# Scores of graph edges: one-hot products for all slots instead of gathers for 54 of them, with GpSimd taking every second group

## The chip, the cores and the metric

The kernel runs on one core of a Trainium2 chip. Its time is the device time of one execution in microseconds (us); smaller is better. The engines are TensorE (PE; its weight loads are shown as PEld), VectorE (DVE), ScalarE (ACT), GpSimd (POOL) and SyncE (SP, which here only issues DMAs). All of them run beside each other and wait for each other by semaphores; each works through its own queue in order. PE writes to PSUM banks, which DVE and ACT can read.

## The reference

Four layers are applied to 1250 nodes with 768 features, each as `x = x + layer(layernorm(x))`: a graph attention with 12 heads, a mixture of 8 experts, a graph attention with 3 relations (two convolutions, of 4 heads and of 1), and an attention block with routing. There are 20,000 edges, sorted by destination. What matters here is the score of an edge, which each of the three graph convolutions needs before its softmax:

```
e = leaky_relu(a1[src] + a2[dst])            # layer 0, 12 heads
qi = xr[etype, dst] @ q;  kj = xr[etype, src] @ k
alpha = leaky_relu(qi + kj)                  # layer 1, 4 heads and 1 head
```

Then come a maximum over each destination's edges, the exponential, the sum over each destination, and the sum of the weighted source rows.

## The kernel before, in words

**Tiles and slots.** Nodes lie in 10 tiles of 128. Edges are packed by destination tile into `NS` = 172 slots of 128 edges. A slot belongs to one destination tile; its sources are anywhere. For each slot there are two rows in DRAM, `lo_rows` (source modulo 128) and `dl_rows` (destination within its tile), and on the chip `hi_f` (source tile) or `key_f` (source tile and relation).

**`edge_weights` (L418 to L617)** computes the scores. It is called three times: g0 for layer 0 (L774), g1 and g2 for the two convolutions of layer 1 (L1211, L1255). It works in blocks of `step` slots, 18 in g0 and g1, 32 in g2. In a block:

- SP loads `row_lo` and `row_dl`, each spread over 128 partitions (L494), and DVE compares them with the partition's number (L495): one-hot matrices in bf16.
- *Source scores, one-hot.* PE multiplies a slot's one-hot matrix with the scores of all source tiles, split into three bf16 parts (L507, `p_al`), so that every edge gets the scores of its source for all 10 tiles (times 3 relations). A group of `ag` = 4 slots (16 in g2) fills a PSUM bank, two groups a pair of banks. DVE multiplies the group with the one-hot choice of the tile, `sel_k` (L473), into `c_al` (L514) and sums over the tiles (L516, `s_a`). A block of 18 slots has five groups: four of 480 columns and one of 240.
- *Source scores, gathered.* Where `al_d` is given (g0 and g1), this is left out for the first `GATHERED` = 54 slots. Their scores are fetched by 54 indirect DMAs of GpSimd (L468, `gal`) from a table in DRAM, which SP writes tile by tile (L718 `al_d`, L1202 `al1_d`). The 118 other slots are done first, the 54 in the last three blocks.
- *Destination scores.* PE multiplies `row_dl` with the scores of the slot's own tile (L523, `p_ar`); ACT and DVE add the three parts into `d_e` (L529 to L531).
- The two are added (L550 for gathered slots, L558 or L560 for the others) and go through the leaky relu into `e` (L566).
- At the third block the penalties that end a segment are made (L403 to L414) and loaded (L539 to L545).
- `fill(beside)` (L567): in g1 and g2 each block also issues products of layer 1's values, `xr` (L1141), one node tile and relation at a time, 24 matmuls each, followed by ACT's copy to `v_r` (L1153) and SP's write to the table (L1154). 20 of them are left for g1 and the stretch behind it.

Behind the blocks come the two scans for the segment maximum and the exponential (L568 to L616), then `aggregate` (L619), whose gathers read the tables.

**Between the experts and g1 (L1192 to L1202)** `combine` gathers each node tile's two expert outputs `y` by GpSimd (L1084) and DVE adds them to `xs` (L1087); the tile is normed, turned by PE and multiplied with the first relation's weights (`xr`, L1141). At the fifth tile (`t == 4`) the weights `wr` of the two other relations are loaded by SP, four DMAs of 1152 KB (L1121), inside `issue_after(added.ins)` (L1197), which orders only instructions of the same engine as `added`, DVE, behind it.

The order of instructions on an engine is set at build time by a scheduler that goes by program order and its own estimates; a queue then runs in that order whatever happens. PSUM has three pairs of banks for `p_al`, `xr` and others, and two single banks for `p_ar`.

Of the kernel before, what the change touches and what calls it, by code (L numbers as in the profile page):

```python
# [8 lines left out]
F32 = mybir.dt.float32  # L9
# [6 lines left out]
N = 1250  # L16
# [3 lines left out]
NREL = 3  # L20
# [23 lines left out]
RUNS = {H0: 18, H1: 6, 1: 2}  # L44
GATHERED = 54
ES = (2 * N + NEXP * 127) // 128
# [24 lines left out]
class Fast:  # L71
# [345 lines left out]

    def edge_weights(self, name, nrel, heads, al, ar, s, al_d=None, bufs=(2, 2),  # L418
                     fill=lambda n: None, beside=0):


# [4 lines left out]
        nk = NT * nrel  # L426
        ng = GATHERED if al_d is not None else 0
        per = RUNS[heads]
        rows = NSP // per
        hr = rows * heads  # L430
        with tc.tile_pool(name=name + "_m", bufs=1) as rp:
# [8 lines left out]
            with tc.tile_pool(name=name + "_w", bufs=1) as wp:  # L440
# [22 lines left out]
                parts(ar, "arp", arp, lambda o, q: o[:, :, q])  # L463
                gal = None
                if ng:
                    gal = wp.tile([128, ng, g], F32, name="gal")
                    for j in range(ng):
                        nc.gpsimd.indirect_dma_start(  # L468
                            out=gal[:, j, :], out_offset=None, in_=al_d,
                            in_offset=bass.IndirectOffsetOnAxis(ap=self.src_i[:, j:j + 1], axis=0))  # L470
                sel = wp.tile([128, NS - ng, nk], BF16, name="sel_k")
                key = (self.hi_f if nrel == 1 else self.key_f)[:, ng:]
                nc.vector.tensor_tensor(sel, self.iota[:, None, :nk].to_broadcast([128, NS - ng, nk]),  # L473
                                        key[:, :, None].to_broadcast([128, NS - ng, nk]), op=ALU.is_equal)
                if nrel > 1:
# [9 lines left out]
                step = 18 if g > 3 else 32  # L485
                for s0 in list(range(ng, NS, step)) + list(range(0, ng, step)):
                    n = min(step, NS - s0)
                    hot = {}
                    for nm, lists in (("lo", self.lo_rows), ("dl", self.dl_rows)):
                        if nm == "lo" and s0 < ng:  # L490
                            continue
                        w = wp.tile([128, step * 128], BF16, name="row_" + nm, bufs=bufs[nm == "dl"])
                        flat = lists[s0:s0 + n].rearrange("s e -> (s e)")
                        nc.sync.dma_start(w[:, :n * 128], flat[None, :].to_broadcast([128, n * 128]))  # L494
                        nc.vector.tensor_scalar(w[:, :n * 128], w[:, :n * 128], self.own, None,  # L495
                                                op0=ALU.is_equal)
                        hot[nm] = w
                    for i, j0 in enumerate(range(0, n if s0 >= ng else 0, ag)):
                        m = min(ag, n - j0)
                        if i % 2 == 0:  # L500
                            pair = self.ps2("p_al")
                        p = pair[:, i % 2]
                        for j in range(j0, j0 + m):
                            lhs = hot["lo"][:, j * 128:(j + 1) * 128]
                            o = p[:, (j - j0) * nk * heads:(j - j0 + 1) * nk * heads]
                            for q in range(3):
                                mark = nc.tensor.matmul(o, lhs, alp[q].rearrange("p h t r -> p (h t r)"),  # L507
                                                        start=q == 0, stop=q == 2)
                        marks.append(mark)
                        c = wp.tile([128, ag, heads, nk], F32, name="c_al", bufs=2)  # L510
                        v = p[:, :m * nk * heads].rearrange("p (s h k) -> p s h k", s=m, h=heads)
                        ss = slice(s0 + j0, s0 + j0 + m)
                        so = slice(s0 + j0 - ng, s0 + j0 + m - ng)
                        nc.vector.tensor_tensor(c[:, :m], v, sel[:, so, None, :].to_broadcast(  # L514
                            [128, m, heads, nk]), op=ALU.mult)
                        nc.vector.tensor_reduce(sa[:, ss], c[:, :m], AX.X, ALU.add)  # L516
                    for j0 in range(0, n, bg):
# [13 lines left out]
                        nc.vector.tensor_add(o, o, v[:, :, 2])  # L531
                    if s0 == ng + 2 * step:
                        with tc.issue_after(marks[-1].ins):
                            self.penalties(heads)
                        pen = self.pen[heads]
                        rows_in = (sep[:, :per * 128], self.sep_rows), (loss[0], pen[0]), (loss[1], pen[1])
                        for i, (dst, src) in enumerate(rows_in):
                            v = src.rearrange("(r b) e -> r (b e)", b=per)
                            nc.sync.dma_start(dst, v[None].to_broadcast([heads, rows, per * 128]))  # L539
                            if i:  # L540
                                c = per * 128 - 1 if i == 1 else 0
                                ends = rp.tile([1, rows], BF16, name=f"ends{i}")
                                nc.sync.dma_start(ends, v[:, c:c + 1].rearrange("r o -> o r"))
                                nc.vector.tensor_copy(edge[:, i - 1],
                                                      ends[:, None, :].to_broadcast([1, heads, rows]))  # L545

                    b = slice(s0, s0 + n)
                    o, db = sa[:, b], d[:, b]
                    if s0 < ng:
                        nc.vector.tensor_add(db if nrel > 1 else o, db, gal[:, b])  # L550
                    if nrel > 1:
                        dv = db.rearrange("p s (r h) -> p s r h", r=nrel)
                        nc.vector.tensor_tensor(dv, dv, rsel[:, b, :, None].to_broadcast(
                            [128, n, nrel, heads]), op=ALU.mult)
                        if s0 < ng:
                            nc.vector.tensor_add(o, dv[:, :, 0], dv[:, :, 1])
                        for r in range(2 if s0 < ng else 0, nrel):
                            nc.vector.tensor_add(o, o, dv[:, :, r])  # L558
                    elif s0 >= ng:
                        nc.vector.tensor_add(o, o, db)  # L560
# [121 lines left out]
    def layer0_values(self, pp):  # L682

        nc, const, wf = self.nc, self.main, self.wf
        self.tab0 = self.dram.tile([N, H0 * (F0 + 1)], F32, name="tab0")
        self.al_d = self.dram.tile([N, H0], F32, name="al_d")
        self.alr = const.tile([128, NT, 2, H0], F32, name="alr0")
# [20 lines left out]
    def node_values(self, v0, t):  # L708
# [6 lines left out]
        for i in range(2):  # L715
            nc.scalar.copy(self.alr[:r, t, i].rearrange("p (b k s) -> p b k s", b=2, k=3),
                           v[:, :, :, 128 + 2 * i:130 + 2 * i])
        nc.sync.dma_start(self.al_d[rows_of(t)], self.alr[:r, t, 0])  # L718
        for b in range(2):
# [41 lines left out]
    def layer0_graph(self):  # L761
        nc, tc = self.nc, self.tc
        hns, self.pen = {}, {}
        with tc.tile_pool(name="g0e", bufs=1) as ep, ExitStack() as path:
            e0 = self.slot_rows(ep, "e0", H0)
            with tc.tile_pool(name="g0p", bufs=1) as pp:
# [5 lines left out]
                for _ in tiles:  # L772
                    pass
                marks = self.edge_weights("g0", 1, H0, self.alr[:, :, 0], self.alr[:, :, 1], e0, self.al_d,  # L774
                                          (4, 6))
                self.layer0_residuals(pp, self.hT0, marks)
# [335 lines left out]

    def load_relations(self, pool, w, bufs, rels=range(NREL), ng=0):

        nc, a = self.nc, self.a
        ws = []
        for r in rels:
            for n, (o, wd) in enumerate(HALF):
                x = ng if r == 0 and n == 0 else 0
                t = pool.tile([128, KD, 384 + x], F32, name="wr0" if x else "wr", bufs=1 if x else bufs)  # L1120
                nc.sync.dma_start(t[:, :, :384], a[w][r].rearrange("(k p) f -> p k f", p=128)[:, :, o:o + wd])  # L1121
                ws.append(t)
# [44 lines left out]
    def layer1_graph(self):  # L1167
        nc, tc, a, xs, dram = self.nc, self.tc, self.a, self.xs, self.dram
        g1, g2 = NREL * H1, NREL
        with ExitStack() as path:  # L1170
# [9 lines left out]
            tab2 = dram.tile([NREL * N, D + 1], F32, name="tab2")  # L1180
            al1_d = dram.tile([N, NREL * H1], F32, name="al1_d")
            al1 = hp.tile([128, NT, g1], F32, name="al1")
# [6 lines left out]
            with tc.tile_pool(name="g1x", bufs=1) as xp:  # L1189
                vs = self.value_rows(xp, H1, F1)  # L1190
                with tc.tile_pool(name="moec", bufs=1) as cp:
                    for t in range(NT + 1):  # L1192
# [3 lines left out]
                        if t == 4:  # L1196
                            with tc.issue_after(added.ins):  # L1197
                                ws += self.load_relations(xp, "L1_gnn_W1", 4, (1, 2))
                        if t:
                            m = rows_of(t - 1)  # L1200
                            self.relation_values(vs, hT, ws, t - 1, 0, H1, F1, tab1, al1, ar1)
                            nc.sync.dma_start(al1_d[m], al1[:ROWS[t - 1], t - 1, :])  # L1202
                moe.close()
# [6 lines left out]
                fill = self.filler(vs, hT, ws, H1, F1, tab1, al1, ar1)  # L1210
                self.edge_weights("g1", NREL, H1, al1, ar1, e1, al1_d, fill=fill, beside=1)  # L1211
                for t in range(NT):
# [1314 lines left out]
```

## Time and profile before

| what | value |
|---|---|
| median of 7 runs | 2313.34 us (2305.57 to 2321.84) |
| the profiled execution's own time | 2315.46 us |
| its span | 2313.4 us |
| PE busy | 2081.5 us, 90% |
| DVE busy | 1253.7 us, 54% |
| POOL busy | 905.7 us, 39% |
| ACT busy | 302.0 us, 13% |
| g0: blocks of slots | 55 to 132 us of the span |
| `y` gathers to the first `xr` | 718 to 737.5 us |
| g1: blocks of slots | 825 to 942 us |
| rest of the fillers, to the next gather | 942 to 1029.8 us |
| g2: blocks of slots | 1381 to 1491 us |

Where the time goes is told by stage, since different engines set the pace in different stages. These are rows of the table by stretch: bounds in us from the span's start, length, then busy time and number of instructions of PE, PEld, DVE, ACT and POOL, the clock granted to PE (1.00 is full), the mean busy share of the 16 DMA engines and GB/s.

```profile
55.00:131.00 76.00, 49.68 (x642) 46.16 (x642) 60.12 (x153) 10.22 (x28) 54.58 (x54) 0.77 0.51 156
...
720.00:800.00 80.00, 65.31 (x224) 39.63 (x225) 42.42 (x92) 12.46 (x26) 28.92 (x37) 0.87 0.49 184
...
870.00:940.00 70.00, 66.71 (x445) 43.10 (x442) 38.32 (x106) 7.16 (x19) 28.75 (x32) 0.98 0.37 103
```

In g0 no engine is busy throughout, in g1 PE nearly is. Other views used further on are the timeline (start, duration, engine, line, operation, and in brackets the idle time of the engine before it with what ended it), the waits (who waited for whom: total, times, longest) and the chain of work that ended last.

### The profile page before, as it was taken

What the parts mean: (1) busy time and instruction counts of PE and PEld (TensorE: products, weight loads), DVE (VectorE), ACT (ScalarE), POOL (GpSimd) and SP (SyncE); (2) the same over time, 40 slices, a digit from 0 to 9 for tenths busy, and PEclk for the clock granted to TensorE, in tenths of its full rate; (3) what the DMA queues carried; (4) which work ended last, traced back from release to release, by engine and by line L of the source; (5) the groups of instructions that cost most, each with busy time, mean ns of one, the idle gap of its engine ahead of it and who ended that gap; (6) DMA issues with size and microseconds to landing.
All of it is one profiled execution on the core that took longest, in us unless ns stands there. A gap on an engine that the chain in (4) does not pass through costs nothing.

```text
span 2313.4 us, 25705 instructions
## 1 busy us (share of the span) xinstructions
PE 2081.5 (90%) x9261; PEld 1306.1 (56%) x9261; DVE 1253.7 (54%) x2548; ACT 302.0 (13%) x619; POOL 905.7 (39%) x930
## 2 busy tenths in 40 slices
PE   4659999779996999979999989989999999999868
PEld 4544445457774656545555546645555555656556
DVE  7877778889714376618667634112456601244371
ACT  3020000112221100100000010000001100122141
POOL 3748888422104154117777610017765000130040
PEclk9779999979997999989999999999999999999889
DMA  6558898589997164539876525339997010420141
GB/s 215 154 177 260 288 314 280 187 308 383 361 317 264 45 197 108 170 128 338 267 229 219 185 88 186 110 116 311 337 318 279 22 51 0 137 101 6 49 134 55
DMA packets 155930, 445.14 MB, mean 192 GB/s; under 512 B 38525, under 2 KB 75762, under 8 KB 154512
## 3 DMA queue, kind: packets, MB, share of 16 engines
q0 software_dynamic: 55200, 252.50, 33.0%
q1 hardware_dynamic: 95488, 178.02, 22.4%
q10 hardware_dynamic: 5104, 12.85, 1.5%
q8 instruction: 77, 1.26, 0.2%
q14 instruction: 61, 0.50, 0.1%
HBM read 381.43 MB, written 61.87 MB: 192 GB/s over the span
## 4 chain that ended last, share of the span: by engine, by line
PE 55%; DMA 5%; DVE 5%; issue 3%; ACT 1%; POOL 1%; SPq 0%; POOLq 0%; DVEq 0%; ACTq 0%
PE xr L1141 18%; PE acc L654 8%; PE acc L656 8%; PE mix L1395 4%; PE pv L1395 3%; PE pk L1558 3%; PE av L1599 2%; PE pl L1569 2%; PE pf L1684 2%; DMA x_mid<-xs 2%; DMA row<-tab,rel_i 1%; PE ph L1675 1%; PE p_al L507 1%; PE pT L1584 1%; PE mix L1508 1%
## 5 line engine op out<-in xcount | busy, mean ns | idle before, releaser
L633 POOL DMA_INDIRECT row<-tab,rel_i x344 | 387.6, 1127 | 351.2 <-DMA tab<-v_r 169.2
L1141 PE MATMUL xr<-wr,hT 128*128 128x384 f32 (+4 forms) x1440 | 488.1, 496 | 7.5 <-DVE c_al L514 3.9
L1141 PEld LDWEIGHTS xr<-wr,hT 128*128 128x128 f32 (+1 forms) x1440 | 268.9, 190 | 198.8 <-issue 42.4
L650 DVE TENSOR_TENSOR msg<-row,e 128x780 f32<-128x780 f32 (+1 forms) x344 | 328.0, 962 | 97.7 <-DMA row<-tab,src_i 48.8
L654 PE MATMUL acc<-msg,hots 128*128 128x390 f32 (+3 forms) x688 | 290.1, 503 | 35.4 <-DVE msg L650 21.3
L656 PE MATMUL acc<-msg,hots 128*128 128x390 f32 (+3 forms) x688 | 283.9, 493 | 0.0
L633 POOL DMA_INDIRECT row<-tab,src_i x172 | 219.6, 1277 | 78.0 <-DVE e L615 25.8
L654 PEld LDWEIGHTS acc<-msg,hots 128*128 128x128 f32 (+1 forms) x688 | 123.5, 189 | 145.6 <-DVE msg L650 51.2
L656 PEld LDWEIGHTS acc<-msg,hots 128*128 128x128 f32 (+1 forms) x688 | 130.8, 191 | 93.6 <-issue 7.8
L1109 DVE CUSTOM_DVE_ANT_0 wjunk<-wrow,qb 128x768 f32<-128x768 f32 x180 | 160.6, 947 | 12.7 <-DMA wrow<-in_L_gnn_W_dram 12.7
L654 PE MATMUL acc<-row,hot 128*128 128x384 f32 (+1 forms) x344 | 140.1, 489 | 8.8 <-DMA row<-tab,rel_i 8.8
L468 POOL DMA_INDIRECT gal<-al_d,src_i x108 | 112.5, 1042 | 79.0 <-issue 54.4
L656 PE MATMUL acc<-row,hot 128*128 128x385 f32 (+1 forms) x344 | 140.0, 489 | 0.0
L1040 PEld LDWEIGHTS ph<-xT,w 128*128 128x128 f32 x864 | 107.0, 196 | 30.0 <-ACT gT L1043 13.9
L638 DVE TENSOR_SCALAR hot<-iota,dloc,e 128x128 f32<-128x128 f32 x172 | 59.9, 354 | 112.1 <-PE acc L656 92.7
L1040 PE MATMUL ph<-xT,w 128*128 128x128 f32 x864 | 114.0, 283 | 5.6 <-DMA w<-in_L_ffn_w_dram 3.8
L1153 ACT COPY v_r<-xr 128x768 f32<-128x768 f32 (+1 forms) x60 | 47.9, 798 | 449.2 <-PE xr L1141 201.3
L1050 PE MATMUL mo<-w,gT 128*128 128x384 f32 x288 | 103.7, 488 | 0.0
L654 PEld LDWEIGHTS acc<-row,hot 128*128 128x128 f32 (+1 forms) x344 | 64.7, 191 | 53.5 <-issue 12.4
L507 PE MATMUL p_al<-alp,row_lo 128*128 128x120 bf16 (+1 forms) x1224 | 68.4, 214 | 29.2 <-DVE c_al L514 13.4
L656 PEld LDWEIGHTS acc<-row,hot 128*128 128x128 f32 (+1 forms) x344 | 65.4, 190 | 46.2 <-issue 2.8
L507 PEld LDWEIGHTS <-row_lo 128*128 128x128 bf16 x1224 | 63.5, 106 | 42.8 <-issue 25.7
(419 smaller groups left out, 2440.1 us busy)
## 6 DMA issues: line engine op xcount, KB each, us to landing
w<-in_L_ffn_w_dram SPq DMA_DIRECT2D x48, 1152.0 KB
wr<-in_L_gnn_W_dram SPq DMA_DIRECT2D x12, 1152.0 KB
wrow<-in_L_gnn_W_dram POOLq DMA_DIRECT2D x36, 384.0 KB, 6.3
tab<-v_r SPq DMA_DIRECT2D x27, 386.0 KB
tab<-v_r SPq DMA_DIRECT2D x27, 384.5 KB
row_dl<-dl_rows SPq DMA_DIRECT2D x18, 576.0 KB
y_d<-y ACTq DMA_DIRECT2D x24, 384.0 KB
row_lo<-lo_rows SPq DMA_DIRECT2D x12, 576.0 KB
```

The source lines that it names most:

```text
L468: nc.gpsimd.indirect_dma_start(out=gal[:, j, :], out_offset=None, in_=al_d, in_offset=bass.IndirectOffsetOnAxis(ap=self.src_i[:, j:j + 1], ...
L507: mark = nc.tensor.matmul(o, lhs, alp[q].rearrange("p h t r -> p (h t r)"), start=q == 0, stop=q == 2)
L633: nc.gpsimd.indirect_dma_start(out=row, out_offset=None, in_=table, in_offset=bass.IndirectOffsetOnAxis(ap=idx[:, s:s + 1], axis=0))
L650: nc.vector.tensor_tensor(msg.rearrange("p (h f) -> p h f", h=heads), row.rearrange("p (h f) -> p h f", h=heads), es[:, :, None].to_broadc ...
L654: nc.tensor.matmul(acc[:r, 0, :cut], hot[:, :r], msg[:, :cut], start=b == 0, stop=b == CAP[t] - 1)
L656: nc.tensor.matmul(acc[:r, 1, :w - cut], hot[:, :r], msg[:, cut:], start=b == 0, stop=b == CAP[t] - 1)
L1040: nc.tensor.matmul(p[:, o], w1[:, k, f * 128:(f + 1) * 128], xT[:, k // 3, (k % 3) * T:(k % 3 + 1) * T], start=k == 0, stop=k == KD - 1)
L1050: nc.tensor.matmul(p[:, n, :w], gT[:, f * T:(f + 1) * T], w2[:, f, o:o + w], start=f == 0, stop=f == 2)
L1109: nc.vector.tensor_tensor_reduce(out=junk, in0=wr, in1=qb[:, i, h, :], scale=1.0, scalar=0.0, op0=ALU.mult, op1=ALU.add, accum_out=out[:, ...
L1141: nc.tensor.matmul(p[:m, n, :w.shape[2]], hT[:, k, rows_of(t)], w[:, k, :], start=k == 0, stop=k == KD - 1)
L1395: self.nc.tensor.matmul(p[:m, n, :384], left(k), ws[n][:, k, :], start=start and k == 0, stop=k == ks - 1)
L1558: nc.tensor.matmul(p[:, :w], wk[o // 3][:, k, (o % 3) * 128:(o % 3 + 1) * 128], hT[:, k, c:c + w], start=k == 0, stop=k == KD - 1)
```

## The change

1. `GATHERED`, the tables `al_d` and `al1_d`, their writes and the gathers `gal` are gone. All 172 slots get their source scores by one-hot products, in their natural order; `sel_k` covers all slots.
2. Of the groups of a block, those with an odd number are copied from PSUM to `c_al` by ACT and multiplied there by GpSimd; the even ones stay with DVE. DVE sums all of them. `c_al` has three buffers instead of two. This holds in g0, g1 and g2.
3. In `load_relations` each weight tile is first written in one element by DVE, queued behind the fifth tile's sum, so that the load has to wait for that write.

```diff
-GATHERED = 54
...
-                for s0 in list(range(ng, NS, step)) + list(range(0, ng, step)):
+                for s0 in range(0, NS, step):
...
-                    for i, j0 in enumerate(range(0, n if s0 >= ng else 0, ag)):
+                    for i, j0 in enumerate(range(0, n, ag)):
...
-                        c = wp.tile([128, ag, heads, nk], F32, name="c_al", bufs=2)
+                        c = wp.tile([128, ag, heads, nk], F32, name="c_al", bufs=3)
...
-                        nc.vector.tensor_tensor(c[:, :m], v, sel[:, so, None, :].to_broadcast(
-                            [128, m, heads, nk]), op=ALU.mult)
+                        if i % 2:
+                            nc.scalar.copy(c[:, :m], v)
+                            v = c[:, :m]
+                        (nc.gpsimd if i % 2 else nc.vector).tensor_tensor(
+                            c[:, :m], v, sel[:, ss, None, :].to_broadcast([128, m, heads, nk]), op=ALU.mult)
                         nc.vector.tensor_reduce(sa[:, ss], c[:, :m], AX.X, ALU.add)
...
-    def load_relations(self, pool, w, bufs, rels=range(NREL), ng=0):
+    def load_relations(self, pool, w, bufs, rels=range(NREL), ng=0, behind=None):
...
+                if behind is not None:
+                    with self.tc.issue_after(behind.ins):
+                        nc.vector.memset(t[:1, 0, :1], 0.0)
                 nc.sync.dma_start(t[:, :, :384], a[w][r].rearrange("(k p) f -> p k f", p=128)[:, :, o:o + wd])
...
-                            with tc.issue_after(added.ins):
-                                ws += self.load_relations(xp, "L1_gnn_W1", 4, (1, 2))
+                                ws += self.load_relations(xp, "L1_gnn_W1", 4, (1, 2), behind=added)
```

## The prediction

> **What bounds** the kernel now: I began with the page (TensorE, "PE", is busy for 90% of the span), then read the chain that ended last, the timeline of the three stages that the change touches, the waits of PE, and the tables by stretch. "g0", "g1" and "g2" are the three calls of `edge_weights`.
>
> In g0 (55 to 132 us) no engine is full; the end is set by the 54 gathers of `gal`. These are lines of the timeline, columns start, duration, engine, line, operation, with the idle time before in brackets:
>
> ```profile
> 126.99 0.94 POOL L468 DMA_INDIRECT gal<-al_d,src_i  x1 [0.30 <-issue]
> 128.24 0.94 POOL L468 DMA_INDIRECT gal<-al_d,src_i  x1 [0.30 <-issue]
> ...
> 124.97 0.44 DVE L531 TENSOR_TENSOR d_e<-d_e,p_ar 128x168 f32<-128x168 f32 x2
> 130.75 0.38 DVE L550 TENSOR_TENSOR s_a<-d_e,gal 128x216 f32<-128x216 f32 x1 [5.33 <-DMA gal<-al_d,src_i]
> 131.17 0.54 DVE L566 SCALAR_TENSOR_TENSOR e<-s_a 128x216 f32<-128x216 f32 x1
> ```
>
> GpSimd (POOL) issues a gather each 1.25 us (0.94 + 0.30) from 58.45 on. VectorE (DVE) is through at 125.4 and waits 5.33 us for the last one. So at most 5.3 us are to be had before DVE itself is late.
>
> In g1 (825 to 942) PE is the bound. Each block of 18 slots ends with one `xr` product of the filler, and ScalarE's copy of it marks the blocks:
>
> ```profile
> 838.38 0.80 ACT L1153 COPY v_r<-xr 128x768 f32<-128x768 f32 x1 [8.75 <-issue]
> 853.76 0.80 ACT L1153 COPY v_r<-xr 128x768 f32<-128x768 f32 x1 [12.46 <-issue]
> 868.39 0.80 ACT L1153 COPY v_r<-xr 128x768 f32<-128x768 f32 x1 [11.61 <-issue]
> 880.01 0.80 ACT L1153 COPY v_r<-xr 128x768 f32<-128x768 f32 x1 [8.22 <-issue]
> 895.80 0.80 ACT L1153 COPY v_r<-xr 128x768 f32<-128x768 f32 x1 [8.81 <-issue]
> 907.42 0.80 ACT L1153 COPY v_r<-xr 128x768 f32<-128x768 f32 x1 [8.54 <-issue]
> 917.13 0.80 ACT L1153 COPY v_r<-xr 128x768 f32<-128x768 f32 x1 [8.31 <-PE p_ar L523]
> 925.41 0.80 ACT L1153 COPY v_r<-xr 128x768 f32<-128x768 f32 x1 [7.17 <-issue]
> 933.68 0.80 ACT L1153 COPY v_r<-xr 128x768 f32<-128x768 f32 x1 [7.17 <-issue]
> ```
>
> An undisturbed block with one-hot source scores takes 11.62 us (868.39 to 880.01, and 895.80 to 907.42), a gathered block 8.27 us. The other three took 15.38, 14.63 and 15.79. From 942 the fillers run on without a gap to 1025.9, and the next stage waits for the last table write. So a microsecond of PE in g1 is a microsecond of the span. In 824.7 to 1025.9 PE was busy 189.26 of 201.20 us: the 11.9 us idle is all that can hide anything.
>
> Between the experts and g1 (718 to 737) the chain of waits starts with a gather:
>
> ```profile
> 719.24 6.67 DMA y<-y_d,pos_i
> ...
> 737.75 9.57 PE xr L1141 x24
> ```
>
> **Part 1**, source scores of 54 more slots in g1: 54 slots of three products; by the blocks, 3 x (11.62 - 8.27) = +10.05 us of PE. What was removed there (54 gathers, 10 writes of `al1_d` of 0.32 us on SP's queue, three adds of 0.38 us on DVE) lay beside PE and gives nothing. `sel_k` for 172 instead of 118 slots costs DVE 5.53 - 3.85 = 1.7 us (g2 and g1 rows) at 808, beside 16 us of `xr`; if that cover went, it would be 1.7 us.
>
> **Part 2**, odd groups through ScalarE and GpSimd, in g1. The slow blocks' excess is 3.76 + 3.01 + 4.17 = 10.9 us, of which the penalties' products (861.9 to 864.2, 2.3 us) stay, so at most 8.7 us can go. PE's waits name the cause:
>
> ```profile
> PE xr L1141 <- DVE c_al L514: 3.9, 3, 2.5
> PE p_al L507 <- DVE c_al L514: 3.1, 1, 3.1
> ```
>
> That is 7.0 us in which PE waits for DVE to empty a bank of scores. At 841.4 DVE stood 1.82 us before a `row_lo` load with an odd group's product queued behind it; ScalarE (11 us busy of 117) would have emptied that bank in about 0.55 us (its 512-column copy of `p_run` takes 0.586). But the even groups of each bank pair stay on DVE. I take 4.0 of the 8.7. So g1 costs +10.05 - 4.0 = +6.0 us, with ends of +1.3 and +10.05.
>
> **Part 3**, g0: GpSimd's gathers go and DVE is what is late next. DVE is busy 60.8 of the 76.7 us between 55.0 and 131.7. Added: three `row_lo` comparisons, 3 x 0.80 = 2.4; reductions of 12 full and 3 half groups, 12 x 0.60 + 3 x 0.35 = 8.25 (back-to-back rows). Products on DVE fall from 26 full and 7 half to 19 and 10: 19 x 0.61 + 10 x 0.36 = 15.2 against 18.4, -3.2. The `gal` adds turn into `d_e` adds of the same 0.37. Net +7.4, busy 68.2. Idle was 15.9, less the gather wait 5.33 = 10.6. With those gaps kept g0 ends at 55.0 + 68.2 + 10.6 = 133.8: +2.1 us. PE's extra 54 x 3 products (12 in 0.71 us, 1.36 at half clock: 10 to 18 us) go into 27 us in which PE was idle here. `sel_k` (+0.6 us) lies before 55, where DVE waits 1.96 us for ScalarE's `alr`; `al_d` writes of 0.32 us leave SP's queue there, at most -0.5 us, taken as nothing.
>
> The gaps: about 4.5 us of the 10.6 belong to the penalties (80 to 85, and waits for their DMA), the other 6 to PE; I take half of those away with the freed banks, -3. Against that stands a new collision. GpSimd's product of 480 columns is not in the trace; its 768-column add takes 1.81 us, so 480/768 of it gives 1.13, I take 1.2. And while GpSimd computes, some DVE instructions stand still:
>
> ```profile
> 2224.87 1.80 POOL L1669 TENSOR_TENSOR xs<-xs,xb 128x768 f32<-128x768 f32 x1 [0.45 <-DVE ln_rs L117]
> 2225.23 1.86 DVE L118 TENSOR_SCALAR hn<-xs,ln_mv,ln_rs 128x768 f32<-128x768 f32 x1
> ...
> 2227.17 1.82 POOL L1669 TENSOR_TENSOR xs<-xs,xb 128x768 f32<-128x768 f32 x1 [0.50 <-DVE hn L118]
> 2227.48 2.33 DVE L1662 TENSOR_TENSOR xs<-xs,ya 128x768 f32<-128x768 f32 x1
> ```
>
> `hn` takes 0.67 us alone, the sum of two SBUF tensors 0.96; here both end only after GpSimd's add, +1.2 and +1.4. A reading of PSUM beside it (L1368, 0.40) was not stretched. So the exposed ones in a block are the two comparisons, the `s_a` add and L566: 2.5 us of some 8. Two products of 1.2 us cover 0.3 of a block; 4 instructions x 0.3 x half a product (0.6) = 0.7 us per block; by the order of the queue (product, reduction, then the exposed ones) I take half, 0.35 x 9.5 = +3.4. Ends: 0, and half a product for each of the 19, +11.4. So g0 costs 2.1 - 3 + 3.4 = +2.5 us, with ends of -3.9 and +13.5.
>
> The Trainium skill, "GPSIMD Engine Reference", section "Engine selection", speaks against this part: elementwise work belongs on VectorE, since GpSimd is about twice as slow with two inputs. The rows agree with the ratio (1.81 against 0.95 us). Followed, the rule would put 19 x 0.61 = 11.6 us back on DVE in g0 and leave out the +3.4: 8.2 us worse here, because GpSimd has nothing else to do in this stage once the gathers are gone.
>
> **Part 4**, the weights behind the fifth sum: in the old kernel the block had no effect: SP issued the four `wr` loads at 717.81, before the first sum at 724.54, and the 16 DMA engines were full (share 1.05, 416 GB/s at 722 to 724) while the first `y` gathers waited 6.67 us to land. Now a one-element DVE write after the fifth sum (741) holds the loads back. Four such writes cost 0.3 us on DVE, hidden by `xr`; behind the waiting loads on SP's queue stands the first `tab` write (749), which may slip some 2 us and has three buffers. First use of these weights is 829.6. With quiet engines a gather lands in 3.8 (`ya`, least) to 4.8 us (`row`, median); the DVE chain behind it moves as a whole. This gives 4.8 - 6.67 = -1.9 us, with ends of 0 and 3.8 - 6.67 = -2.9.
>
> g2 gets five odd groups and no more slots; PE runs `xr` there for 15 us at a stretch: 0.
>
> **Sum**: +6.0 + 2.5 - 1.9 = +6.6. On the profiled execution (span 2313.4, 2.06 around it, 2315.46) that is 2322; on the median of seven, 2313.34, it is 2320, and that is my number.
>
> **Rivals**:
> *The gaps close.* ScalarE frees the banks early, so g1's three slow blocks become normal (+1.3), g0 loses all 6 us of gaps and meets no collision (2.1 - 6 = -3.9), and the gather lands in 3.8 (-2.9): -5.5, 2308. For it: the 7.0 us of PE's waits on DVE. Against it: every bank pair keeps an even group on DVE, whose queue still waits for loads. It decides from the point where g1's excess over 11.62 us per block is under 2 us in all.
> *The shared access.* GpSimd's products stop DVE at L495, L566 and the adds for half a product each time in g0, +11.4, and DVE then empties banks no sooner in g1, so nothing is recovered: 10.05 + 13.5 - 1.9 = +21.7, 2335. For it: the two stretched rows. Against it: the products fall where DVE reduces. It decides once L495 in g0 has a mean over 1.1 us (now 0.80).
> *The held-back loads give nothing,* since the DVE chain of the first two tiles (726 to 736) is reordered or the loads now cross the later gathers: forecast + 1.9 = 2322.
>
> **Chances**: forecast 0.47, gaps close 0.25, shared access 0.20, loads give nothing 0.08. The forecast's own range is 2314 to 2326. A difference of 0.3% (6.9 us) is about what can be told from no change: under 2306.4 lies somewhat less than half of "gaps close" (0.11); over 2320.3 lie half of the forecast, all of "shared access", most of the last (0.48); between them 0.41. The range 2306 to 2332 leaves out about a tenth on each side.
>
> **Checks**: right are ten blocks of 11.6 us or more in g1, but for the short last one; the first gather after g1 6.6 us later than 1029.8; last L566 of g0 at 133 to 136; the first `y` landing in under 5.2 us. Wrong would be g1 blocks of 10 us, g0 ending before 129, or a stretched DVE op while GpSimd is idle.

## The result, and the profile after

The changed kernel takes 2324.86 us (median of 18 runs, 2317.49 to 2332.67) against 2313.28 us of the kernel before (46 runs beside them): ratio 1.0055, 95% interval 1.0042 to 1.0068, so +12.7 us (+9.7 to +15.7). The forecast was +6.6. The profiled execution took 2326.39 us, its span is 2324.7.

Line numbers after the change are lower by 9 to 16: `row_lo` is compared at L483, `p_al` is L495, ScalarE's copy L503, the product `c_al` L505, its sum L507, `p_ar` L514, `e` L553, the row gathers L620, `xr` L1129, `v_r` L1141.

**g0.** Rows of the table by stretch (columns as before: bounds, length, busy time and count of PE, PEld, DVE, ACT, POOL, clock, DMA share, GB/s), then waits of DVE in g0 (total, times, longest; the first two lines before, the other two after), then the timeline where the scores end and where the row gathers begin:

```profile
56.00:139.90 83.90, 54.35 (x753) 49.79 (x754) 67.72 (x168) 17.26 (x43) 20.81 (x19) 0.78 0.39 128
...
870.00:940.00 70.00, 69.70 (x589) 47.92 (x587) 46.44 (x117) 13.87 (x31) 12.70 (x12) 1.00 0.34 118
```

```profile
DVE c_al L514 <- PE p_al L507: 5.9, 9, 1.1
DVE s_a L550 <- DMA gal<-al_d,src_i: 5.3, 1, 5.3
...
DVE s_a L507 <- POOL c_al L505: 9.9, 13, 1.8
DVE c_al L505 <- PE p_al L495: 2.4, 3, 1.7
```

```profile
138.31 0.65 DVE L507 TENSOR_REDUCE s_a<-c_al 128x48 f32<-128x480 f32 x1 [0.95 <-POOL c_al L505]
139.00 0.28 DVE L547 TENSOR_TENSOR s_a<-s_a,d_e 128x120 f32<-128x120 f32 x1
139.32 0.37 DVE L553 SCALAR_TENSOR_TENSOR e<-s_a 128x120 f32<-128x120 f32 x1
```

```profile
168.57 1.78 POOL L1083 DMA_DIRECT2D qb<-in_L_gnn_q_dram  x3 [26.68 <-DVE e L602]
170.66 1.04 POOL L620 DMA_INDIRECT row<-tab,src_i  x1 [0.30 <-ACT e L603]
```

The last score is ready at 139.7 in place of 131.7 us. In place of one wait of 5.33 us for a gather, DVE now waits 13 times for a product of GpSimd, 9.9 us in all. The first row gather goes out 11.0 us later than before (170.66 against 159.64): 8.0 us of this lie ahead of the last score and 3.0 behind it, where among others three loads of `qb` now stand ahead of the gather.

**g1.** PE is busy for 69.70 of 70 us at the full clock (second row above). The fillers' copies, as in the prediction:

```profile
868.48 0.80 ACT L1141 COPY v_r<-xr 128x768 f32<-128x768 f32 x1 [8.85 <-PE xr L1129]
880.04 0.80 ACT L1141 COPY v_r<-xr 128x768 f32<-128x768 f32 x1 [6.59 <-PE xr L1129]
891.60 0.80 ACT L1141 COPY v_r<-xr 128x768 f32<-128x768 f32 x1 [6.59 <-PE xr L1129]
903.15 0.80 ACT L1141 COPY v_r<-xr 128x768 f32<-128x768 f32 x1 [6.59 <-PE xr L1129]
```

From 868 to 938 each block takes 11.56 us; there is no block of 8.3 any more, and only the first three are longer (13.58, 12.32, 15.07).

**The `y` gathers**, issue to landing; least, median and most were 6.0, 6.7 and 7.4 before:

```profile
DMA to landing us min/median/max: 3.7/4.7/8.9
```

### The profile page after: what moved, and what is told of

Read it like the earlier page. It is cut to its first block, busy times and chain, and to the rows that moved or that the text cites. A ratio compares the mean times of both kernels' runs of the same rounds, so it can differ in the third digit from the quotient of the medians.

```text
span 2324.7 us, 26287 instructions
## 1 busy us (share of the span) xinstructions
PE 2096.5 (90%) x9585; PEld 1324.2 (57%) x9585; DVE 1271.7 (55%) x2575; ACT 326.4 (14%) x662; POOL 835.0 (36%) x865
## 4 chain that ended last, share of the span: by engine, by line
PE 56%; DVE 5%; DMA 5%; issue 2%; ACT 1%; POOL 1%; SPq 0%; DVEq 0%; ACTq 0%; POOLq 0%
PE xr L1129 19%; PE acc L643 7%; PE acc L641 7%; PE mix L1379 4%; PE pv L1379 3%; PE pk L1542 3%; DMA x_mid<-xs 2%; DMA row<-tab,rel_i 2%; PE av L1583 2%; PE pl L1553 2%; PE pf L1668 2%; PE ph L1659 1%; PE p_al L495 1%; PE mix L1492 1%; PE pT L1568 1%
## 5 line engine op out<-in xcount | busy, mean ns | idle before, releaser
L1129 PE MATMUL xr<-wr,hT 128*128 128x384 f32 (+4 forms) x1440 | 487.1, 495 | 4.5 <-DVE hT L139 3.3
L620 POOL DMA_INDIRECT row<-tab,rel_i x344 | 390.8, 1136 | 258.2 <-DMA tab<-v_r 74.6
L1129 PEld LDWEIGHTS xr<-wr,hT 128*128 128x128 f32 (+1 forms) x1440 | 267.7, 189 | 195.5 <-issue 42.2
L620 POOL DMA_INDIRECT row<-tab,src_i x172 | 212.4, 1235 | 52.4 <-issue 27.4
L1093 DVE CUSTOM_DVE_ANT_0 wjunk<-wrow,qb 128x768 f32<-128x768 f32 x180 | 160.8, 951 | 11.4 <-DMA wrow<-in_L_gnn_W_dram 11.4
L505 POOL TENSOR_TENSOR c_al<-c_al,sel_k 128x480 f32<-128x480 f32 x43 | 46.4, 1079 | 280.4 <-ACT c_al L503 280.4
L495 PE MATMUL p_al<-alp,row_lo 128*128 128x120 bf16 (+1 forms) x1548 | 88.8, 215 | 36.0 <-DVE row_lo L483 21.1
L495 PEld LDWEIGHTS <-row_lo 128*128 128x128 bf16 x1548 | 82.2, 104 | 52.9 <-issue 24.4
L1141 ACT COPY v_r<-xr 128x768 f32<-128x768 f32 (+1 forms) x60 | 48.0, 799 | 423.3 <-PE xr L1129 264.9
L1034 PE MATMUL mo<-w,gT 128*128 128x384 f32 x288 | 103.8, 489 | 0.0
```

What stands on the lines that cost most here:

```text
L620: nc.gpsimd.indirect_dma_start(out=row, out_offset=None, in_=table, in_offset=bass.IndirectOffsetOnAxis(ap=idx[:, s:s + 1], axis=0))
L1034: nc.tensor.matmul(p[:, n, :w], gT[:, f * T:(f + 1) * T], w2[:, f, o:o + w], start=f == 0, stop=f == 2)
L1093: nc.vector.tensor_tensor_reduce(out=junk, in0=wr, in1=qb[:, i, h, :], scale=1.0, scalar=0.0, op0=ALU.mult, op1=ALU.add, accum_out=out[:, ...
L1129: nc.tensor.matmul(p[:m, n, :w.shape[2]], hT[:, k, rows_of(t)], w[:, k, :], start=k == 0, stop=k == KD - 1)
```

## The experiments

Each experiment's kernel was run 6 to 12 times beside 17 to 30 runs of the kernel before on the same chip. The ratio is to those, with its 95% interval; in us it is taken of 2313.3. The stages are read from one profiled execution each, in us: first row gather of layer 0 (g0 and its scans end there); from it to the first `y` gather; from that to the last product of the first relation, and from that to the last of the 20 fillers (g1), both taken at the start of ScalarE's copy of it; from the next gather, some 5 us later, to the end.

| kernel | row gather | to `y` | to last r = 0 | fillers | rest | ratio |
|---|---|---|---|---|---|---|
| before | 159.6 | 558.4 | 106.7 | 200.3 | 1283.6 | 1 |
| changed | 170.7 | 552.6 | 104.2 | 204.0 | 1288.5 | 1.0055 (1.0042-1.0068) |
| e1, weights alone | 161.2 | 559.5 | 104.3 | 199.1 | 1286.4 | 0.9972 (0.9950-0.9995) |
| e2, no gathers, all on DVE | 170.4 | 559.1 | 103.9 | 205.6 | 1289.8 | 1.0055 (1.0034-1.0077) |
| e3, g0 gathered | 160.2 | 556.7 | 104.9 | 204.6 | 1288.4 | 1.0006 (0.9986-1.0026) |
| e4, both gathered, GpSimd too | 161.2 | 545.1 | 104.6 | 250.1 | 1284.7 | 1.0199 (1.0163-1.0235) |
| e6, sums later | 170.3 | 548.9 | 104.2 | 204.1 | 1286.8 | 1.0025 (1.0004-1.0046) |
| e7, q and k loads behind | 174.2 | 554.2 | 105.2 | 203.8 | 1283.0 | 1.0071 (1.0044-1.0098) |
| e8, ScalarE copies | 162.2 | 557.2 | 104.2 | 194.4 | 1284.2 | 0.9986 (0.9964-1.0008) |
| e10, 36 gathered in g0 | 161.1 | 556.6 | 104.4 | 200.0 | 1282.2 | 0.9986 (0.9965-1.0008) |
| e11, rows ahead | 171.5 | 549.8 | 104.6 | 204.5 | 1283.3 | 1.0045 (1.0022-1.0067) |
| e12, 90 gathered in g1 | 163.4 | 557.3 | 103.8 | 217.2 | 1284.4 | 1.0085 (1.0060-1.0110) |
| e13, 108 gathered in g1 | 163.2 | 561.0 | 103.7 | 239.7 | 1287.6 | 1.0143 (1.0115-1.0170) |
| e14, 72 gathered in g1 | 161.2 | 550.5 | 105.0 | 197.1 | 1289.6 | 0.9976 (0.9958-0.9994) |

Read the columns for how far one execution can be trusted. "To `y`" holds work that the edits leave alone, yet it lies between 545 and 561, and "rest" between 1282 and 1290. The third and fourth columns repeat to 1.5 us among kernels with the same stage. The first does to 1.6 us in the four profiles with g0 as it was (before, e1, e3, e4; their last scores lie at 131.7 to 133.3 us), but not in g0 as changed: e7 leaves g0's instructions alone, VectorE and GpSimd run them in the same order there, and its last score comes at 143.2 us in place of 139.7. So differences of some 3.5 us at the last score are not told apart among the kernels without gathers. And the tail's +4.9 us in the changed kernel's trace, and the 5.8 us that it seems to win back before `y`, are within this scatter.

**e1, the third part alone.**

```diff
+                if behind is not None:
+                    with self.tc.issue_after(behind.ins):
+                        nc.vector.memset(t[:1, 0, :1], 0.0)
```

> The kernel before with the third part of the change alone: the two relations' weights wait for a one-element write behind the fifth tile's sum. Forecast: -1.9 us against the kernel before, 2311.4 us. From the trace of the changed kernel (first y gather landing in 3.7 to 4.7 us in place of 6.7; distance from the first y gather to the last product of the first relation 106.7 -> 104.2): -2.5 us, 2310.8 us. Rival, the loads give nothing (the products of the first relation bound the stretch anyway): 0, 2313.3 us.

Measured: 2307.94 us, -6.5 (-11.6 to -1.2) by the ratio, which holds both expected gains and excludes zero. The stage gives the size: 106.7 became 104.3, and all thirteen kernels with this part lie between 103.7 and 105.2. The part gains 2.3 us, and the rival is out.

**e2, the second part undone.** All products on DVE, no gathers; the third buffer of `c_al` stays. Against the changed kernel:

```diff
-                        if i % 2:
-                            nc.scalar.copy(c[:, :m], v)
-                            v = c[:, :m]
-                        (nc.gpsimd if i % 2 else nc.vector).tensor_tensor(
+                        nc.vector.tensor_tensor(
```

> The changed kernel without GpSimd's half: no slot is gathered, all products stay on VectorE (three c_al buffers kept), weights behind the fifth sum. Forecast (its parts 2 and 3): g1 +4.0 and g0 +8.2 against the changed kernel, 2337 us. Theory after the trace: in g0 VectorE now loses 9.9 us waiting for GpSimd's products, so about 11.6 us of products come back and 9.9 us of waits go, +1.7 there; in g1 the stalls of 7.3 us come back; 2325 + 9 = 2334 us, and the last score of g0 ends at 139 to 142 us. Rival, the odd groups' detour gives nothing in g1 either (the stalls went with the gathers, whose traffic held up the row_lo loads): 2325 to 2327 us.

Measured: 2326.19 us, the same ratio as the changed kernel. In g0 DVE's table row, to be laid beside that of the changed kernel:

```profile
56.00:141.90 85.90, 53.05 (x751) 48.78 (x752) 76.75 (x186) 6.57 (x26) 0.00 (x0) 0.78 0.37 126
```

GpSimd takes 9 us of work off DVE (76.75 to 67.72 us). Of this nothing is shown at the end: the last score comes at 142.2 us, between the 139.7 and 143.2 of the two profiles with the changed g0, and the first row gather at 170.4 (170.7 and 174.2). In g1 the detour is worth 205.6 - 204.2 = 1.4 us (204.2 is the mean of the five kernels with it, 203.8 to 204.6; 205.6 is one profile). The forecast's 8.2 and 4.0 are both refuted; the time is that of the rival.

**e3, g0 put back**, with the 54 gathers of `gal` in g0, and g1 as changed. Against the kernel before:

```diff
-        ng = GATHERED if al_d is not None else 0
+        ng = {"g0": 54, "g1": 0, "g2": 0}[name]
...
+                        odd = i % 2 and name != "g0"
+                        if odd:
+                            nc.scalar.copy(c[:, :m], v)
+                            v = c[:, :m]
```

> The changed kernel with g0 as it was before (54 gathered slots, all products on VectorE); in g1 and g2 no gathers and odd groups through ScalarE and GpSimd; weights behind the fifth sum. Theory: g0's scores cost the changed kernel +8 us at their end, +11 at the first row gather and +5.3 at the first y gather; with g0 as before these go: 2325 - 5.3 = 2319.5 us, first y gather at 718. Rival A, g0's delay is absorbed before the experts end and the loss sits in g1 and behind it: 2324 us. Rival B, the delay is carried in full: 2325 - 11 = 2314 us.

Measured: 2316.49 us. Against the changed kernel the ratio falls by 0.0049, 11.3 us (some 5.5 either way). That is nearest to rival B: g0's delay of 10.5 us at the row gather (170.7 against 160.2) is carried to the end. So g0 is most of the loss.

**e4, gathers and products on GpSimd together in g1** (e3 with 54 gathered slots in g1 too):

```diff
+        ng = {"g0": 54, "g1": 54, "g2": 0}[name]
```

> As the run with g0 as before, but in g1 too the 54 gathered slots are kept, with the odd groups of the 118 others through ScalarE and GpSimd; weights behind the fifth sum. Theory: the stalls of PE in g1 are those of VectorE's order and go with the detour, 7.3 us, while the 10.05 us of extra products are not paid: kernel before - 2.5 - 7.3 = 2303.5 us, blocks of 11.6 and 8.3 us in g1. Rival, the stalls belong to the gathers (their traffic holds up row_lo loads, and GpSimd, busy issuing them, holds up the products): 2311 us, with long blocks left in g1.

Measured: 2359.23 us, +46 (+38 to +54). Both theories missed. The waits in g1, then GpSimd's timeline:

```profile
PE p_al L507 <- DVE c_al L518: 51.9, 2, 50.1
```

```profile
DVE s_a L520 <- POOL c_al L518: 48.8, 10, 42.4
```

```profile
887.45 0.94 POOL L468 DMA_INDIRECT gal<-al_d,src_i  x1 [0.30 <-issue]
888.41 3.08 POOL L518 TENSOR_TENSOR c_al<-c_al,sel_k 128x480 f32<-128x480 f32 x3
```

The first product stands in GpSimd's queue behind 54 gathers; DVE waits 42.4 us for it, and PE 50.1 us for DVE. So the second part of the change needs the first: the gathers have to leave before GpSimd can help.

**e6, sums later in g0.** An odd group's sum goes behind the next even group's product and sum.

```diff
+                        if i % 2 and nrel == 1:
+                            late.append((ss, m, c))
+                            continue
...
+                            with tc.issue_after(prod.ins):
+                                nc.vector.tensor_reduce(sa[:, qs], qc[:, :qm], AX.X, ALU.add)
```

> The changed kernel, where in g0 VectorE sums an odd group only behind the next even group's product and sum (a fourth c_al buffer in g0 makes room), so that GpSimd has that long to finish. Theory: g0 is late because VectorE's queue stands still before these sums (9.9 us in the changed kernel's trace between 54 and 140 us); most of that goes: last score of g0 at 133 to 135 in place of 139.7 us, first row gather at 164 to 166, time 2325 - 4 to 6 = 2320 us. Rival, VectorE only paces the same chain as PE and ScalarE (PE waits 4.5 us for ScalarE's copies and 10.6 us for row_lo), so the idle time moves to another row: last score at 138 to 140 us, 2325 us.

Measured: 2318.86 us; last score at 140.95, row gather at 170.3. DVE still waits 7.4 us for GpSimd, and for PE 3.6 in place of 2.4. The stage says rival: 133 to 135 us is missed by far. The time lies 0.0030 of ratio under the changed kernel, 7 us, with some 5.7 either way, and its trace shows no place in g0 or g1 for that; it is not explained.

**e7, q and k loads behind the tenth row gather.**

```diff
+                with self.tc.issue_after(self.tenth.ins):
                     nc.gpsimd.dma_start(qb[:, i, h, :], a[n][h:h + 1, :].to_broadcast([128, D]))
```

> The changed kernel, where the eight loads of layer 1's q and k rows on GpSimd's queue are ordered behind the tenth row gather of layer 0; in the changed kernel three of them stand ahead of the first row gather and take 2.1 us. Theory: first row gather at 168.6 in place of 170.7 us, and as PE stands still until the first rows land, that carries to the first y gather: 2323 us. Rival, the loads only change places (the stretch of the 172 row gathers is bound by the gathers themselves, and the loads cost GpSimd the same later): 2325 us.

Measured: 2327.72 us, row gather at 174.2 us. This told nothing of the loads: the scheduler put three `wrow` loads of the same 1.78 us in the place that came free, and from the last score to the row gather it is 31.0 us as in the changed kernel (27.9 before). What the 2.1 us ahead of the gathers are worth stays open. What the run does show is the scatter of g0's end, said above.

**e11, comparisons two blocks ahead in g0.**

```diff
+                    if s0 + ahead * step < NS:
+                        hots[s0 + ahead * step] = rows_of_block(s0 + ahead * step)
```

> The changed kernel, where in g0 a block's row_lo and row_dl are loaded and compared two blocks ahead of their use in program order. Theory: what paces g0 is not one engine's work but the turn between VectorE and PE at each block: PE waits 10.6 us in three long waits for the comparison of the next row_lo, which stands in VectorE's queue behind sums that wait for GpSimd; with the comparisons ahead those go, last score at 131 to 135 in place of 139.7 us, 2320 us. Rival, PE's waiting there costs nothing, since VectorE's own queue (68 us of work and 10 us of waits for GpSimd) is the pace: last score at 138 to 141 us, 2325 us.

Measured: 2321.74 us; last score at 142.56, row gather at 171.5. PE's waits for `row_lo` (10.6 us) are gone, and these stand in their place, first of DVE, then of PE:

```profile
DVE s_a L516 <- POOL c_al L514: 14.0, 16, 1.3
```

```profile
PE p_al L504 <- DVE c_al L514: 16.3, 8, 3.2
```

My theory fell a second time: the wait moved and g0 ended no sooner than in the two profiles of the changed g0. Rival.

**e8, ScalarE's copy without GpSimd**, gathers as before, weights behind the fifth sum, three buffers of `c_al`:

```diff
+                        if i % 2:
+                            nc.scalar.copy(c[:, :m], v)
+                            v = c[:, :m]
                         nc.vector.tensor_tensor(c[:, :m], v, sel[:, so, None, :].to_broadcast(
```

> The kernel before with the weights behind the fifth sum, 54 gathered slots in g0 and g1 as before, and odd groups only copied from PSUM by ScalarE (three c_al buffers); VectorE multiplies all groups, GpSimd none. Theory: what PE waited for in g1 was VectorE emptying banks of scores (7.0 us); ScalarE empties half of them: 3 to 5 us less than with the weights alone, 2304 to 2306 us, and the 20 fillers of g1 take 195 to 197 us from the last product of the first relation in place of 199.1 to 200.3. Rival, the long blocks go with the gathers and not with the banks: 199 us there, 2308 to 2311 us.

Measured: fillers in 194.4 us, 4.7 less than e1, as the theory had it. Of PE's waits for DVE's products in g1 this is left (in e1 3.8 and 2.0):

```profile
PE p_al L507 <- DVE c_al L517: 2.9, 2, 1.8
```

The 4.7 us are more than the waits that went. Over the stretch of the fillers PE is idle for 7.7 us in place of e1's 9.9, and busy for 186.7 in place of 189.3 us with the same 1050 products: 2.6 us are the same work run faster, at a granted clock of 1.00 in place of 0.98. Where the clock was lost shows in the kernel before, right behind its two longest waits of PE for DVE (2.48 us, to 843.4, and 3.08 us, to 884.4):

```profile
844.00:846.00 2.00, 2.00 (x14) 1.27 (x13) 1.07 (x2) 0.00 (x0) 1.70 (x2) 0.50 0.28 81
...
884.00:886.00 2.00, 1.62 (x17) 1.62 (x17) 1.20 (x3) 0.00 (x0) 1.39 (x3) 0.55 0.03 3
```

In e8 no wait of PE among the blocks is longer than 1.83 us, and the clock is 1.00 through all of them. In e2 and in the changed kernel, whose longest waits there are shorter still, it is 1.00 too; in e1, with waits of 2.42 and 2.00 us, it falls again (0.72 from 843 to 849). So a long wait that goes gives back more than itself, as far as these traces tell. Whether the third buffer alone would do some of this was not run.

The time, 2309.13 us, is not told apart from e1's (ratios 0.9986 and 0.9972, each some 0.0022 either way), so the stage's gain is shown, and that of the whole is not.

**e10, 36 gathered slots in g0**, on top of e1:

```diff
-        ng = GATHERED if al_d is not None else 0
+        ng = {"g0": 36, "g1": 54, "g2": 0}[name]
```

> The kernel before with the weights behind the fifth sum and 36 gathered slots in g0 in place of 54 (g1 keeps 54; all products on VectorE). Theory from the forecast's own sum: VectorE gets a third of 7.4 us, the gathers end 18 x 1.25 = 22 us earlier, so VectorE ends g0 at 125.4 + 2.5 + 1 = 129 in place of 131.7: 2305 to 2309 us. Rival from the run without any gather and without GpSimd's products (last score at 141.8): each block that is not gathered costs (141.8 - 126) / 3 = 5 us, last score at 131 to 132: 2308 to 2311 us.

Measured: 2309.85 us, last score at 132.7 us (before 131.7, e1 133.2). The score is nearer the rival's 131 to 132 than the theory's 129; the time does not tell the two apart. DVE waits for no gather any more (4.1 us in e1), yet the score comes only 0.5 us sooner than in e1. So by these two profiles the one block more that is multiplied cost about 3.6 us, where a third of the forecast's 7.4 is 2.5.

**e12, e13 and e14, more gathers in g1** (90, 108 and 72 for `"g1"` in the same line), on top of e8.

> The opposite direction in g1: the kernel before with the weights behind the fifth sum, ScalarE's copies of odd groups, 54 gathered slots in g0 and 90 in place of 54 in g1. Theory: g1's scores have some 50 us to spare (the next stage waits for the last filler's table write at 1022 us and not for the scores), so gathers there cost PE nothing, and each block of 18 gathered instead of multiplied saves 11.6 - 8.3 = 3.3 us: 6.6 us less than the run with ScalarE's copies, fillers in 188 us, 2302 us. Rival, 36 more gathers at 1.25 us each hold up the end of g1 (last gather issued at 817 + 112 = 930, behind which PE waits in the gathered blocks), nothing gained: 2309 us.

> As the run before it with 108 gathered slots in g1. Theory: the last gather is issued at 817 + 135 = 952 us, the two scans and the exponential behind it take some 30 us and end before the last filler at 1008: a further 3.3 us less, fillers in 185 us, 2299 us. Rival, the late gathers stop PE or delay the first row gather beyond the last table write: 2303 us or more.

> As the run with 90 gathered slots in g1, with 72. There PE waited 26.6 us for the last scores, since the gathers began at 830.6 and the last was issued at 949.6 us, while PE reached the turning of the scores at 938. Theory: with 18 gathers fewer (about 1.33 us each) the last is issued at 926 and the last scores are ready at some 930 us, before PE comes to them, so one more block at 8.3 in place of 11.6 us is a plain gain over ScalarE's copies alone: fillers in 191 us in place of 194.4, 2304 to 2306 us, the fastest of all and below the kernel before. Rival, PE still waits for the last gathers, or the gain is lost behind g1: fillers in 194 us or more, 2309 us or more.

Measured: 2333.09, 2348.30 and 2307.41 us; fillers in 217.2, 239.7 and 197.1 us. In e12 PE reached the turning of the scores for the scan, which stands in its queue ahead of the remaining fillers, and waited:

```profile
PE p_run L580 <- DVE e L569: 26.6, 1, 26.6
```

The scores had time to spare only by the table write, not by PE's queue. With 72 PE still waits there (1.2 us) and for the scans (3.6 and 2.2), and the block saved is lost again: 197.1 is above e8's 194.4. Yet e14 and e1 are the two whose interval lies under 1: -5.6 us (-9.7 to -1.4) and -6.5 us (-11.6 to -1.2). Both beat the kernel before and the changed one; between the two the runs don't decide.

## Why the prediction was right in sign, and where its terms were off

- *Part 1, +10.05 in g1:* right. All blocks but the first three and the last are 11.56 us, where three were 8.27.
- *Part 2, -4.0 in g1:* the fillers' stretch grew from 199.8 (mean of before, e1, e10) to 204.2, so -5.7 was won back. That g1 came out near the forecast (+4.4 for +6.0) is luck: 4.2 of the 5.7 came in e2, which has neither ScalarE's copies nor GpSimd's products but no gathers and a third buffer, and only 1.4 from the detour that was forecast to give 4.0. Why PE's waits for DVE are shorter without gathers (4.0 us in e2, 5.8 in e1, 7.0 before) is not shown. Part of the slow blocks' excess was no wait at all: it was PE at half its clock behind the two longest waits (e8's rows), which the sum did not know of. That the waits for banks were a real cause is shown by e8, 5.4 us under the same mean with gathers in place (the third buffer came with it).
- *Part 3, +2.5 in g0:* this is the step that failed. At the last score +8.0, at the first row gather +11.0 (by the scatter told above, 6 to 12 and 9 to 15 between any two profiles). Three of its numbers held: DVE's busy time 67.7 (forecast 68.2), GpSimd's product 1.10 us (1.13 worked out, 1.2 taken), ScalarE's copy 0.56 us (0.55). DVE's waits for PE fell by 3.5 (5.9 to 2.4; forecast 3). What was wrong is the collision. I priced it at +3.4, as DVE instructions stretched by GpSimd. In its place stands DVE's wait for the products, 9.9 us, which the sum had no term for: a sum queued on DVE behind a copy (0.56) and a product (1.10) on two other engines. DVE's queue adds up so: busy +6.9, waits for GpSimd +9.9, for the gather -5.3, for PE -3.5, others -0.8, together 7.2 us, and it began 1.0 us later. In g0 the changed kernel has:

```profile
L505 POOL TENSOR_TENSOR c_al<-c_al,sel_k 128x480 f32<-128x480 f32 x19 | 20.8, 1095 | 83.7 <-ACT c_al L503 83.7
...
L483 DVE TENSOR_SCALAR row_lo<-row_lo,own 128x2304 bf16<-128x2304 bf16 x6 | 4.9, 812 | 0.0
```

  The stretching that I feared had hardly anything to stretch. By the times of the trace none of the 14 comparisons (0.81 us; before 0.85, and 0.82 for `row_dl`) and none of the 10 adds of `s_a` (0.378 us at most; before 0.380) in this stretch lies beside a product of GpSimd: during the products DVE mostly summed, multiplied from PSUM or waited. Two of the ten L553 do, at 0.54 us as alone. One copy of `edge_t`, 0.18 us alone, does too, and ended with the product:

```profile
97.22 1.08 POOL L505 TENSOR_TENSOR c_al<-c_al,sel_k 128x480 f32<-128x480 f32 x1 [0.88 <-ACT c_al L503]
...
97.81 0.53 DVE L535 COPY edge_t<-ends 1x120 bf16<-1x120 bf16 x1
```

  That is +0.35 us for the 3.4. A smaller term was missing too: 3.0 us lie between the last score and the first row gather (27.9 us in all four profiles with g0 as it was, 31.0 in the changed kernel and e7; `qb` loads 2.1; the residuals' products, now among the scans, about 1). The first product of DVE starts 2.0 us later as well (60.04 against 58.05); but e1, with g0 as it was, starts it at 60.46, so that the longer `sel_k` did this is not shown.
- *The rule that I set against part 3* (the Trainium skill, "GPSIMD Engine Reference", section "Engine selection": elementwise work belongs on VectorE) stood against my 8.2 us, and those were wrong: e2 follows the rule and is no slower. It is no faster either, so this case shows no harm in breaking it.
- *Part 4, -1.9:* right, -2.3. g2 at 0: "rest" is 1285.8 on average in the six kernels with GpSimd in g2, and 1285.5 in before, e1, e2 and e10.
- *Sum by the stages:* +10.5 (e3's stage and ratio) + 4.4 - 2.3 = +12.6 against +12.7 measured. The checks named ahead came out as: blocks in g1 right, `y` landing right, last score at 133 to 136 wrong (139.7). The first gather behind g1 came 6.4 us late for a forecast 6.6, which is right by accident: that execution had won back 5.8 us of g0's delay ahead of `y`.
- *Rivals:* "the gaps close" fails, since g1's excess stayed at 6.1 us (2.0 of it in the first block, which the forecast's 10.9 left out) and g0 ended late. "The shared access" fails by its price, +0.35 us for 11.4. Its own mark, L483 at 0.81 for a bound of 1.1, could not decide it, since no comparison met a product. "The loads give nothing" fails.
- *Left open:* what paces g0 without gathers. The scores need 79.7 us (e7 81.3) from the first product with GpSimd and 81.2 without (e2), so the 9.9 us of waits are not by themselves what makes g0 late; moving sums (e6) or comparisons (e11) moved the idle time between rows and ended nothing sooner. PE, DVE and the clock (0.50 at 119 to 126 us, where PE was busy 2.9 of 7.1 us, and 1.00 at 134 to 140) are all part of that loop, and no run separates them.

## What to carry to other kernels

Work given to another engine whose result returns to the same in-order queue is priced by that queue's wait for the result, not by the busy time taken away: here 9 us of work left VectorE, 9.9 us of waits came, and g0 is not shown to end sooner than with all the work on VectorE. A price for two engines stopping each other needs a count of the instructions that will meet, and the order of the queues decides that: one was slowed here. Take a combined change apart before judging it: its smallest part (-2.3 us) was the only one whose gain reached the time. And before an idle engine is given a latency-bound job, see what already stands in its queue.

## What was unexpected of the hardware

GpSimd and VectorE do stop each other, but only where certain instructions meet. In e4, in g1, an add of two SBUF tensors that takes 0.22 us alone met a product of GpSimd and ended just behind it:

```profile
897.04 1.06 POOL L518 TENSOR_TENSOR c_al<-c_al,sel_k 128x480 f32<-128x480 f32 x1 [0.97 <-ACT c_al L516]
...
897.23 0.96 DVE L562 TENSOR_TENSOR s_a<-s_a,d_e 128x72 f32<-128x72 f32 x1
...
898.68 0.22 DVE L562 TENSOR_TENSOR s_a<-s_a,d_e 128x72 f32<-128x72 f32 x1
```

The sums over 480 columns are not slowed: 0.64 us for the ten beside a product in the changed g0, 0.65 for the 28 others. The Trainium skill ("SBUF — State Buffer", section "SBUF: two separate sides") says that GpSimd and a DVE instruction with two SBUF inputs lock each other out for a whole instruction, whichever starts first. The add agrees. The other way round it is not seen in full: two of the changed kernel's 43 products began 0.1 us behind an L553 with two SBUF inputs, lay beside it for 0.44 us and took 1.24 and 1.25 us, where the other 41 took 1.05 to 1.10, so they lost less than 0.2 us. Three products back to back took 3.08 us in e4, 1.03 each, which confirms the length of one by spacing. Of the clock: in g0 it is granted at 0.76 to 0.78 on average with gathers and without, and a `p_al` product takes 251 ns on average there in the changed kernel, against 215 over the whole of it; in g1 it fell to 0.50 and 0.55 behind two waits of PE (e8's rows).
